# Modulation gates of a transformer block: from a matmul broadcast to a DRAM write and broadcast reads

## The chip, the cores and the metric

The kernel runs on one core of one Trainium2 chip. A core has five engines that each work through their own instructions in order: TensorE (PE: matmuls, and PEld, its weight loads), VectorE (DVE), ScalarE (ACT), GpSimd (POOL) and SyncE (SP, which here only issues transfers). The metric is the device time of one execution in microseconds (us).

## The reference

Input x is (4, 1024, 256) in float32, with a conditioning vector `mod` (4, 256) and a context of 77 tokens per batch. Two layers follow each other. The first is a block modulated by nine vectors per batch:

```python
m = silu(mod) @ w_ada + b_ada
sh_msa, sc_msa, g_msa, sh_mca, sc_mca, g_mca, sh_mlp, sc_mlp, g_mlp = [m[:, i*C:(i+1)*C][:, None, :] for i in range(9)]
x = x + g_msa * _self_attn(_ln(x) * (1 + sc_msa) + sh_msa, ...)         # windows of 128, 16 heads of 16
x = x + g_mca * _topk_cross_attn(_ln(x) * (1 + sc_mca) + sh_mca, ...)   # the 16 largest of 77 scores
x = x + g_mlp * _swiglu(_ln(x) * (1 + sc_mlp) + sh_mlp, ...)            # hidden width 1024
```

The second layer is another cross attention behind a layer norm with scale and bias from the same vector; it has no gate. The three gates g_msa, g_mca and g_mlp (each 256 numbers per batch) are what this change is about: each ends a branch with `h @ W + b`, so the kernel multiplies W's columns and b by the gate once per batch, and the branch then needs no product of its own.

## The kernel before

**Tiling.** The 4 batches are cut into 4 units of 256 rows (two row tiles of 128). Each of the 16 units passes five stages: self attention, selection (the 16 largest scores), cross attention, mlp, last attention. Units overlap: while one unit's selection keeps VectorE busy, another's mlp keeps PE busy.

**Order.** The program is written as a list of operations (`Plan.op`: engine, modelled cost, the closure that issues the instructions, buffers read and written, priority). `Plan.place` puts them one by one on the engines in modelled time, by priorities from hand-tuned tables, and gives every operation its buffers out of rings; `Plan.issue` then calls the closures in this order. So each engine's order is fixed when the program is built, and every engine runs its queue in that order; semaphores make an instruction wait for those on other engines whose results it reads or whose buffers it overwrites. The order depends on the modelled costs and the engine named in `op`, not on what a closure really issues.

**Start.** Before the first unit can run, the nine modulation vectors are made: `mod_group` (L690) makes shifts and scales as columns in the tile `mod` (added at L718), and `mod_gate` (L721) makes the three gates as rows: a matmul (L727) and VectorE's addition of the bias (L730) leave them in `gates`, a tile of 4 partitions (one for each batch) with 3 x 256 numbers. `context_columns` (copies by ScalarE at L755) and `context_kv` prepare keys and values of the context.

**The gates' way to 128 partitions.** `gated(b, pr)` (L1292) is called once for each batch b, and for each of three pairs of weights and bias: `w_so`, `w_co` (128 x 512 numbers each) and `w_m2` (128 x 2048). It

- loads the weights and the bias row, the latter broadcast to 128 partitions, by SP (L592);
- on PE, multiplies a broadcast column of the identity by `gates` (L1303), which writes row b of the gate to all 128 partitions of a PSUM bank (`mm`, a ring of two that nearly all matmul results go through; the profile shows two records for each of these matmuls, a pair);
- on ScalarE, copies the bank to the tile `gate` (L1306), a ring of two;
- on POOL, multiplies the bias row by it (L1308) and then the weights (L1310), in place.

That makes 12 matmuls, 12 copies and 24 multiplications in the whole kernel. The times at which the 12 matmuls start in the profiled execution (us): 34.45, 37.28, 38.95 and 42.1 (batch 0, and the first of batch 1), 89.9, 103.7, 117.5, 271.3, 336.1, 507.3, 527.8, 563.4.

**Other lines that the prediction speaks of.** In `normed` (layer norm): POOL's L907 and L909 (variance plus epsilon, power of -0.5: `rs`), VectorE's L912 (normalized rows), PE's transposes L919. In `self_attention`: the value projection L1075, scores and their shifts L1098 and L1104. In `shifts`: POOL's L961 (the first of four small operations on the negated row maxima `nm`, which VectorE's L996 makes), PE's transposes L970. In `norm` (softmax denominators): ScalarE's L1008, POOL's L1011 and L1023. L1049 (`add_row`) adds a gated bias row to x on POOL. L1162 is VectorE's sum in the selection stage.

Of the kernel before, what the change touches and what calls it, by code (L numbers as in the profile page):

```python
# [9 lines left out]
F32 = mybir.dt.float32  # L10
BF16 = mybir.dt.bfloat16
AF = mybir.ActivationFunctionType
ALU = mybir.AluOpType
# [3 lines left out]
P = 128  # L17
# [371 lines left out]
def tile_block(ctx: ExitStack, tc: tile.TileContext, a: dict, out: bass.AP):  # L389
    nc = tc.nc  # L390

    x_d, cond_d, ctx_d = a["x"], a["cond_1024"], a["ctx_1024"]
    B, L, C = x_d.shape
# [16 lines left out]
    def ctile(shape, name, dt=F32):  # L410
        return const.tile(shape, dt, tag=name, name=name)
# [7 lines left out]
    ident = ctile([P, P], "ident")  # L419
# [37 lines left out]
    pl = Plan()  # L457


    def f_pe(cols, n):  # L460
        return n * (cols * 0.00175 + 0.0095) + 0.1

    def f_act(n):
        return 0.21 + 0.00081 * n

    def f_dve(n):
        return 0.155 + 0.00104 * n

    def f_pool(n):
        return 0.13 + 0.00222 * n  # L470
# [7 lines left out]
    T_GATE = ("D", "D", 0.22, 0.05, 0.37, 0.216)  # L478
# [11 lines left out]
    def fixed(name, shape, dt=F32):  # L490
        return pl.fixed(ctile(shape, name, dt), name)
# [8 lines left out]
    n_mod = 26  # L500
    mod = fixed("mod", [P, n_mod, B])
    gates = fixed("gates", [B, 3, C])
    k_ctx = [fixed(f"k_{i}", [P, KC, B, 2, LC]) for i in range(2)]
    v_ctx = [fixed(f"v_{i}", [LC, B, H // 2, VP]) for i in range(2)]
    for v, fill in zip(v_ctx, (0.0, 1.0)):
# [7 lines left out]
    start, total = {}, 0  # L513
# [52 lines left out]
    bg_ada = at.buf("bg_ada", [B, 3, C])  # L566
# [22 lines left out]
    def load(buf, src, kb, prio, key=None, eng="SP", view=None):  # L589
        def fn():  # L590
            dst = buf() if view is None else view(buf())
            (nc.sync if eng == "SP" else nc.scalar).dma_start(dst, src)  # L592
        pl.op(eng, f_dma(kb) if eng == "SP" else 0.3, fn, w=[buf if key is None else (buf, key)],
              prio=prio, lag=2.0)
# [21 lines left out]
    for g, names in enumerate(groups):  # L616
        for name, hi in names:
            n, r = hi // P, n_rows[g]
# [11 lines left out]
    def chunk(name, lo, n, prio):  # L630
        c = pl.buf("chunk", f"{name}{lo}")
        load(c, a[name].rearrange("(kc p) n -> p kc n", p=P)[:, :, lo : lo + n], n, prio,
             view=lambda t: t[:, :, :n])
        early.append((chunk_lo, chunk_hi, c))
        return c
# [85 lines left out]
    def mod_gate(i, prio, dma_prio):  # L721
        c = chunk("L0_xcond_w_ada", (3 * i + 2) * C, C, dma_prio)
        pp = pl.buf("mm", f"modg{i}")

        def fn():
            for kc in range(KC):
                nc.tensor.matmul(pp()[:B, :C], sc_t()[:, kc, :B], c()[:, kc, :C],  # L727
                                 start=(kc == 0), stop=(kc == KC - 1))
        pl.op("PE", f_pe(C, 2), fn, w=[pp], r=[sc_t, c], prio=prio)
        pl.op("DVE", f_dve(256), lambda: nc.vector.tensor_tensor(  # L730
            gates()[:, i, :], pp()[:B, :C], bg_ada()[:, i, :], ALU.add), w=[(gates, i)], r=[pp, (bg_ada, i)], prio=prio)

    def filled(v):

# [55 lines left out]
    for i, key in enumerate("kqv"):  # L790
        weight(w_qkv, "L0_xcond_w_qkv", -84 + i, (1, 0, 2)[i] * C, C, key)
    mod_gate(0, -30, -79)
    mod_group("L0_xcond_w_ada", 3 * C, 6, False, -3, -70)
    load(cx, ctx_d.rearrange("b k c -> k b c"), 308, -69)
    weight(w_kv[0], "L0_xcond_w_kv", -68)
    weight(w_q0, "L0_xcond_w_q", -67)
    mod_gate(1, -2, -59)
    mod_group("L0_xcond_w_ada", 6 * C, 12, False, -1, -50)
    mod_gate(2, -1, -49)
    mod_group("L1_xcond_Wss_q", 0, 18, True, -1, -48)  # L800
    mod_group("L1_xcond_Wss_kv", 0, 22, True, -1, -47)
# [9 lines left out]
    for b in range(B):  # L811
        pl.op("DVE", 0.42, lambda b=b: nc.vector.bn_stats(st_c()[:LC, b, :], cx()[:, b, :]),
              w=[(st_c, b)], r=[cx], prio=-1)
    for b in range(B):
        pl.op("DVE", 0.16, lambda b=b: nc.vector.bn_aggr(mv_c()[:LC, b, :], st_c()[:LC, b, :]),
              w=[(mv_c, b)], r=[(st_c, b)], prio=-1)
# [475 lines left out]
    def gated(b, pr):  # L1292

        gw = {}
        for i, (key, name, kc) in enumerate(
            (("so", "L0_xcond_w_so", KC), ("co", "L0_xcond_w_co", KC), ("m2", "L0_xcond_w_m2", NF))
        ):
            first = None if b else DMA_FIRST[i]
            w, row = pl.buf("w_" + key, f"w_{key}{b}"), pl.buf("row", f"b_{key}{b}")
            gate, pg = pl.buf("gate", f"gate{b}{i}"), pl.buf("mm", f"pg{b}{i}")  # L1300
            load(w, a[name].rearrange("(kc p) n -> p kc n", p=P), 128 * kc, first or pr)
            load(row, a[f"L0_xcond_b_{key}"].partition_broadcast(P), 128, first or pr)
            pl.op("PE:gate", T_GATE, lambda i=i, pg=pg: nc.tensor.matmul(  # L1303
                pg()[:, :C], ident[:B, b : b + 1].to_broadcast([B, P]), gates()[:, i, :], start=True, stop=True),
                w=[pg], r=[(gates, i)], prio=pr, take=[gate])
            pl.op("ACT:gate", f_act(256), lambda gate=gate, pg=pg: nc.scalar.copy(gate(), pg()[:, :C]),  # L1306
                  w=[gate], r=[pg], prio=pr)
            pl.op("POOL:gate", f_pool(256), lambda row=row, gate=gate: nc.gpsimd.tensor_tensor(  # L1308
                row(), row(), gate(), ALU.mult), w=[row], r=[row, gate], prio=pr)
            pl.op("POOL:gate", f_pool(256 * kc), lambda w=w, gate=gate, kc=kc: nc.gpsimd.tensor_tensor(  # L1310
                w(), w(), gate().unsqueeze(1).to_broadcast([P, kc, C]), ALU.mult),
                w=[w], r=[w, gate], prio=pr)
            gw["b_" + key], gw["w_" + key] = row, w
        return gw

    stages = (self_attention, selection, cross_attention, mlp, last_attention)
    for b in range(B):
        pl.at = None
        gw = gated(b, b * NU - 0.5)
        for part in range(NU):  # L1320
            u = Unit()
            u.b, u.part, u.name = b, part, f"_{b}{part}"
            u.prio = float(b * NU + part)
            pl.at = None
            u.x = pl.buf("x", "x" + u.name)
            move_x(u, x_d, False)
            for k, stage in enumerate(stages):
                pl.at = (b * NU + part, k)
                u.prio = ORDER[b * NU + part][k]
                stage(u, gw)  # L1330
# [45 lines left out]
```

## Time and profile before

| | us |
|---|---|
| median of 3 runs (lowest, highest) | 1042.11 (1041.72, 1042.24) |
| the profiled execution's own time | 1041.43 |
| its span, from the first to the last instruction | 1039.4 |
| POOL's 12 multiplications L1308, each | 0.72 |
| POOL's 12 multiplications L1310: w_so and w_co, w_m2 | 1.26 to 1.27, 4.51 to 4.54 |
| the mean granted clock of PE over the span | 0.993 |

The page of the profile gives, in this order: each engine's busy time with its share of the span and the number of instructions; the span in 40 equal slices (26 us each here), one digit for each, in tenths; the transfers; the chain of work that ended last; and the costliest groups of instructions, with the idle time of the engine in front of them and what ended it. In a list of single instructions (the timeline) a line holds start, duration, engine, source line, operation, output<-inputs and shapes; a bracket at its end gives the engine's idle time in front of it and what released it. SPq is an issue in SP's queue. In the chain of waits a line holds start, duration, engine, tile and source line.

The only transfers of this kernel are issued by SP and, for a few small rows at the very start, by ScalarE; POOL issues none.

### The profile page before, as it was taken

How to read it: one execution, taken by the hardware profiler on the slowest of the kernel's cores; microseconds unless marked ns; L12 is line 12 of the kernel's file. 1: busy time of each engine (PE TensorE's matmuls, PEld its weight loads, DVE VectorE, ACT ScalarE, POOL GpSimd, SP SyncE). 2: the span in 40 equal slices, each digit the busy share in tenths (PEclk: the TensorE clock that was granted, in tenths of full speed). 3: DMA queues.
4: the chain of work that ended last, by engine and by line, in shares of the span. 5: the costliest groups of instructions: out<-in, count | busy, mean ns of one | idle time of the engine just before them, and what ended most of it. 6: DMA issues, size and time to landing. Idle time of an engine off the chain costs nothing.

```text
span 1039.4 us, 27476 instructions
## 1 busy us (share of the span) xinstructions
PE 1012.0 (97%) x10363; PEld 770.5 (74%) x10363; DVE 757.3 (73%) x4000; ACT 723.5 (70%) x1270; POOL 542.1 (52%) x751
## 2 busy tenths in 40 slices
PE   7899999999999999999999999999999999999997
PEld 5667777777777778777877777778767787778775
DVE  5177999979899999947833446599999977724232
ACT  3358786687687794758468667877688765764665
POOL 3384445466353573557635647546335464753653
PEclk9799999999999999999999999999999999999999
DMA  7710000001000000100000200000000001000000
GB/s 255 242 50 7 3 2 1 3 3 36 3 22 27 7 3 5 38 16 22 21 1 2 82 22 21 2 2 2 2 2 22 2 2 42 12 1 12 2 21 21
DMA packets 23623, 27.01 MB, mean 26 GB/s; under 512 B 1609, under 2 KB 20675, under 8 KB 23491
## 3 DMA queue, kind: packets, MB, share of 16 engines
q1 hardware_dynamic: 23455, 25.26, 7.7%
q8 instruction: 81, 1.33, 0.5%
q14 instruction: 52, 0.42, 0.1%
q10 hardware_dynamic: 35, 0.01, 0.0%
HBM read 21.07 MB, written 4.19 MB: 24 GB/s over the span
## 4 chain that ended last, share of the span: by engine, by line
PE 48%; DVE 13%; ACT 6%; POOL 2%; issue 1%; POOLq 0%; ACTq 0%; DVEq 0%
PE mm L1247 13%; PE mm L1275 8%; PE mm L938 5%; PE mm L1035 5%; PE s L1196 4%; PE o L1212 3%; PE s L985 3%; DVE share L1153 2%; DVE r L1147 2%; DVE nm L996 2%; PE s L1186 1%; DVE share L1145 1%; DVE share L1151 1%; PE mm L919 1%; ACT prob L1108 1%
## 5 line engine op out<-in xcount | busy, mean ns | idle before, releaser
L1247 PE MATMUL mm<-share,w_m 128*128 128x256 f32 x640 | 150.3, 386 | 0.4 <-ACT share L926 0.2
L1205 ACT ACTIVATE prob<-s 77x2048 f32<-77x2048 f32 x64 | 120.0, 1875 | 43.7 <-PE s L1201 43.4
L996 DVE TENSOR_REDUCE nm<-s 128x16 f32<-128x2048 f32 (+1 forms) x64 | 119.0, 1859 | 38.0 <-PE s L985 17.2
L1247 PEld LDWEIGHTS mm<-share,w_m 128*128 128x128 f32 x640 | 117.7, 190 | 26.0 <-issue 4.7
L1147 DVE MATCH_REPLACE8 r<-share 128x77 f32<-128x77 f32 x512 | 109.9, 222 | 0.0
L1145 DVE MAX8 share<-share 128x8 f32<-128x77 f32 x512 | 94.4, 225 | 21.0 <-ACT share L1138 21.0
L1153 DVE MATCH_REPLACE8 share<-share,r 128x77 f32<-128x77 f32 x512 | 109.6, 221 | 0.0
L1011 POOL TENSOR_TENSOR share<-share 128x256 f32<-128x256 f32 x64 | 47.1, 736 | 96.4 <-ACT share L1008 95.1
L1151 DVE MAX8 share<-r 128x8 f32<-128x77 f32 x512 | 93.9, 224 | 0.0
L1247 PE MATMUL mm<-slab,w_m 128*128 128x256 f32 x384 | 92.9, 388 | 0.7 <-ACT slab L926 0.5
L1023 POOL TENSOR_TENSOR slab<-slab,share 128x256 f32<-128x256 f32 x96 | 69.4, 730 | 28.4 <-ACT share L1018 19.2
L1261 POOL TENSOR_SCALAR slab<-slab 128x512 f32<-128x512 f32 x43 | 64.4, 1498 | 36.8 <-ACT slab L1259 33.0
L1247 PEld LDWEIGHTS mm<-slab,w_m 128*128 128x128 f32 x384 | 69.9, 190 | 15.6 <-issue 3.1
L1275 PE MATMUL mm<-share,slab 128*128 128x256 f32 x344 | 80.9, 381 | 0.0
L1008 ACT ACTIVATE share<-o,mask 128x256 f32<-128x256 f32 x128 | 66.6, 575 | 12.2 <-PE o L1212 9.6
L1108 ACT ACTIVATE prob<-s 128x2048 f32<-128x2048 f32 x32 | 60.5, 1889 | 17.9 <-PE s L1104 17.5
L1044 DVE TENSOR_TENSOR slab<-slab,mm 128x512 f32<-128x512 f32 x52 | 35.4, 680 | 50.9 <-PE mm L1035 25.7
L1275 PEld LDWEIGHTS mm<-share,slab 128*128 128x128 f32 x344 | 64.7, 190 | 10.0 <-issue 0.9
L1253 ACT ACTIVATE slab<-mm,cols 128x256 f32<-128x256 f32 x90 | 43.0, 480 | 41.0 <-PE mm L1247 40.5
L1212 PE MATMUL o<-prob,v 77*32 77x256 f32 x1024 | 67.9, 385 | 0.8 <-ACT share L1018 0.5
L1049 POOL TENSOR_TENSOR slab<-slab,row 128x512 f32<-128x512 f32 x39 | 49.9, 1278 | 28.5 <-DVE slab L912 15.4
L907 POOL TENSOR_SCALAR rs<-mv 128x2 f32<-128x2 f32 x64 | 14.2, 222 | 81.7 <-DVE mv L905 78.8
(183 smaller groups left out, 2427.0 us busy)
## 6 DMA issues: line engine op xcount, KB each, us to landing
share<-in_L_xcond_w_m_dram SPq DMA_DIRECT2D x4, 1024.0 KB
slab<-in_x_dram SPq DMA_DIRECT2D x9, 256.0 KB, 2.9
out_dram<-slab SPq DMA_DIRECT2D x9, 256.0 KB, 2.7
w_m<-in_L_xcond_w_m_dram SPq DMA_DIRECT2D x4, 512.0 KB, 6.8
share<-in_L_xcond_w_ada_dram SPq DMA_DIRECT2D x3, 512.0 KB, 3.8
w_so<-in_L_xcond_w_so_dram SPq DMA_DIRECT2D x4, 256.0 KB
w_co<-in_L_xcond_w_co_dram SPq DMA_DIRECT2D x4, 256.0 KB, 4.0
w_qkv<-in_L_xcond_w_qkv_dram SPq DMA_DIRECT2D x3, 256.0 KB
```

What stands on the lines that cost most here:

```text
L996: pl.op("DVE:max", f_dve(n), lambda: nc.vector.tensor_reduce(nm()[:, t], s4(), AX.X, ALU.max, negate=True), w=[(nm, t)], r=[s], prio=u.prio)
L1008: pl.op("ACT:nln", 0.5, lambda e=e, own=own, other=other: nc.scalar.activation(nz()[:, e, :], o()[:, ts(e, UT)], AF.Ln, bias=own, scale=ot ...
L1023: nc.gpsimd.tensor_tensor(dst, dst, shaped(nz()[:, k, :], dst), op)
L1108: pl.op("ACT:exp", f_act(2048), lambda s=s, prob=prob: nc.scalar.activation(prob(), s(), AF.Exp), w=[prob], r=[s], prio=pr)
L1145: nc.vector.max(top()[:, h + i, 0:8], sc()[:, h + i])
L1147: nc.vector.match_replace(r1()[:, i], top()[:, h + i, 0:8], sc()[:, h + i], NEG)
L1151: nc.vector.max(top()[:, h + i, 8:16], r1()[:, i])
L1153: nc.vector.match_replace(sc()[:, h + i], top()[:, h + i, 8:16], r1()[:, i], NEG)
L1205: pl.op("ACT:exp", f_act(2048), lambda s=s, prob=prob: nc.scalar.activation(prob()[:LC], s()[:LC], AF.Exp), w=[prob], r=[s], prio=pr)
L1212: nc.tensor.matmul(o()[r, :UT] if drops is not None else o()[r, ts(e, UT)], columns(v_z()[:, b], 8 * c + 2 * j + e), prob()[:LC, j, ts(e, ...
L1247: nc.tensor.matmul(pp()[:, ts(half, UT)], w_m1()[:, kc, m : m + P], ht()[:, kc, :], start=(kc == 0), stop=(kc == KC - 1))
L1275: nc.tensor.matmul(pp()[:, ts(t, C)], gts[f // 2]()[:, f % 2, ts(t, P)], w_m2()[:, f, :], start=(f == 0), stop=(f == NF - 1))
```

## The change

The PE closure in `gated` no longer issues a matmul, and ScalarE's copies are gone. In their place, each gate is written to outer memory as soon as VectorE has made it, and is read back from there to all 128 partitions straight into the tile `gate`; POOL issues both the writes and the reads.

```diff
@@ -500,6 +500,9 @@
     gates = fixed("gates", [B, 3, C])
+
+    dram = ctx.enter_context(tc.tile_pool(name="dram", bufs=1, space=bass.MemoryType.DRAM))
+    gates_d = [dram.tile([B, C], F32, tag=f"gates_d{i}", name=f"gates_d{i}") for i in range(3)]
@@ -727,8 +730,11 @@
-        pl.op("DVE", f_dve(256), lambda: nc.vector.tensor_tensor(
-            gates()[:, i, :], pp()[:B, :C], bg_ada()[:, i, :], ALU.add), w=[(gates, i)], r=[pp, (bg_ada, i)], prio=prio)
+
+        def add():
+            nc.vector.tensor_tensor(gates()[:, i, :], pp()[:B, :C], bg_ada()[:, i, :], ALU.add)
+            nc.gpsimd.dma_start(gates_d[i], gates()[:, i, :])
+        pl.op("DVE", f_dve(256), add, w=[(gates, i)], r=[pp, (bg_ada, i)], prio=prio)
@@ -1300,11 +1306,11 @@
-            pl.op("PE:gate", T_GATE, lambda i=i, pg=pg: nc.tensor.matmul(
-                pg()[:, :C], ident[:B, b : b + 1].to_broadcast([B, P]), gates()[:, i, :], start=True, stop=True),
+
+            pl.op("PE:gate", T_GATE, lambda i=i, gate=gate: nc.gpsimd.dma_start(
+                gate(), gates_d[i][b, :].partition_broadcast(P)),
                 w=[pg], r=[(gates, i)], prio=pr, take=[gate])
-            pl.op("ACT:gate", f_act(256), lambda gate=gate, pg=pg: nc.scalar.copy(gate(), pg()[:, :C]),
-                  w=[gate], r=[pg], prio=pr)
+            pl.op("ACT:gate", f_act(256), lambda: None, w=[gate], r=[pg], prio=pr)
```

Engines, costs, priorities and buffers named in `op` stay as they were, so the planned order is the same. In the instruction streams, PE loses 12 matmuls and ScalarE 12 copies; VectorE's and SP's stay as they are; POOL gains 15 issues of transfers, 3 writes (4 x 256 numbers) and 12 reads (256 numbers to 128 partitions). The reads stand in POOL's stream where the planner had put the matmuls in its modelled time. For batch 0 this gives: write 0, long before the rest; then writes 1 and 2; the read of gate 0, its row and w_so; the reads of gates 1 and 2; their row and w_co; an addition of a row to x (L1049); the first read of batch 1; w_m2 and its row. Of the later reads, most stand one to five instructions in front of the multiplication that uses them. Lines behind the change have numbers that are 3 higher (from L503 on) and 6 higher (from L736 on).

## The prediction

> **What bounds the kernel now.** I read the page first, then the chain of waits by window, then the timeline around each of the twelve places that the diff touches.
>
> ```profile
> PE 1012.0 (97%) x10363; PEld 770.5 (74%) x10363; DVE 757.3 (73%) x4000; ACT 723.5 (70%) x1270; POOL 542.1 (52%) x751
> ...
> PE   7899999999999999999999999999999999999997
> PEclk9799999999999999999999999999999999999999
> DMA  7710000001000000100000200000000001000000
> ```
>
> PE is busy nearly everywhere; POOL, which takes on the new work, half the time. But a busy PE need not set the end: for that I look at the chain. It can be followed back to about 300 us only, so only for the four gate matmul pairs after that (336, 507, 528 and 563 us) does it say which of them count. Two windows of the chain, start, us, what:
>
> ```profile
> 336.34 0.32 DVE zz L1162
> 336.66 2.20 DVE nm L996
> ```
>
> ```profile
> 527.88 0.62 PE mm L1303 x2
> 528.50 0.59 PE mm L919 x4
> ```
>
> At 336 us the chain is in VectorE's selection work, though L1303 runs on PE at 336.08; at 507 us too; at 563 us it is in ScalarE. Only the pair at 527.88 is a link. Before 300 us VectorE is busy 93.4 of 96 us (104 to 200) and 86.8 of 100 us (200 to 300), and the pairs at 89.9, 103.7 and 271.3 us are followed by a matmul that waits for ScalarE or VectorE in any case (0.33, 0.58 and 0.26 us). I count nothing there.
>
> The start is another matter. The windows table (us; PE, PEld, DVE, ACT, POOL busy; granted clock; DMA share; GB/s):
>
> ```profile
> 35.10:38.50 3.40, 2.50 (x11) 1.62 (x11) 0.00 (x0) 2.93 (x9) 1.94 (x2) 0.50 0.96 336
> 41.95:45.36 3.41, 3.41 (x15) 2.40 (x9) 0.00 (x0) 2.14 (x2) 3.23 (x2) 0.50 1.02 348
> 45.36:48.77 3.41, 3.41 (x36) 2.54 (x39) 1.27 (x3) 0.00 (x0) 2.17 (x2) 0.50 0.80 243
> 48.77:52.20 3.43, 3.43 (x63) 2.46 (x52) 1.03 (x6) 2.98 (x4) 0.11 (x1) 1.00 0.73 178
> ```
>
> From 35.1 to 48.77 us PE runs at half clock, without gaps from 38.9 on, VectorE waits for it (12.7 us for the matmul of L1075), and the transfers are saturated. Here PE sets the pace, and POOL and the transfers get new work in the same microseconds.
>
> **Removed: 12 matmul pairs (L1303) and 12 copies (L1306).** At full clock a pair is 0.6 us (0.62 on the chain), at half clock 0.9: L1104 ends at 42.31 and L1075 starts at 43.20; the pair at 38.95 stretches the 32 matmuls of L1098 to 2.92 us, where the next 32 take 2.04. The pairs at 34.45 and 37.28 lie in front of matmuls that wait for mod (L718) and for the bank that L755 empties until 38.45, so they are worth nothing. Start: 0.89 + 0.88 = **1.8 us** earlier at L1075. Chain at 528: **0.6 us**. The 12 copies (0.37 each) are off the chain in every window; what waits for them is POOL (22.4 us in six waits), which then waits for the transfer instead.
>
> **Added on POOL: 3 stores and 12 broadcast reads.** No instruction of before issues a transfer from POOL. Let c be POOL's time for one issue and l the time from its end until the data may be used. For c the nearest rows are SP's issue of a like row (0.34) and a POOL pass over 128x512 (1.27); I take 1.0, nearer to the POOL row, since POOL's cheapest pass over this very tile is 0.72. For l in quiet stretches there is a row: SP issues w_co at 331.22 for 0.37, POOL starts on it at 333.96, so l = 2.4. Under load, the bias rows land 4.6 us after issue (4.1 after its end), and one 9.3; those stand behind SP's own backlog, and the new queue has none, so I take 3.2, between 2.4 and 4.1.
>
> The transfer's cost is POOL's, since POOL runs in order: everything behind a multiplication that waits for its gate is late. Batch 0, POOL's new order: store 1, store 2, read 0, row, w_so, read 1, read 2, row, w_co, x + row (L1049), read of batch 1, w_m2, row. Store 0 goes out at 11.8 us, with POOL idle until 20.7: free. Store 2 can't start before VectorE's L730 ends (31.37). Issues on the path: store 2, read 0, read 1, read of batch 1 (4c; read 2 runs under the landing of read 1). Landings: read 0 and read 1 (2l). Work: 0.72 + 1.26 + 0.72 + 1.27 + 1.26 + 4.51 + 0.72 = 10.46. POOL is through at 31.37 + 10.46 + 4c + 2l = **41.8 + 4c + 2l** = 52.2 us. Before it was through at 47.5:
>
> ```profile
> 42.11 1.16 PE L1303 MATMUL mm<-gates,ident 4*128 4x256 f32 x2
> 43.20 3.78 PE L1075 MATMUL mm<-w_qkv,slab 128*128 128x256 f32 x8
> 46.80 0.72 POOL L1308 TENSOR_TENSOR row<-row,gate 128x256 f32<-128x256 f32 x1
> 52.09 0.73 POOL L1011 TENSOR_TENSOR share<-share 128x256 f32<-128x256 f32 x1 [4.56 <-ACT share L1008]
> 54.91 0.72 DVE L912 TENSOR_SCALAR slab<-slab,mv,rs 128x256 f32<-128x256 f32 x2
> ```
>
> The 4.56 us of idle time in front of L1011 are the cover. Behind it stand L1011, L907 and L909 (1.83 us with gaps), and VectorE's L912 at 54.91 needs them: POOL may be through at 53.1 without harm to the old times. With PE 1.8 us earlier, all of the start can move by min(1.8, 53.1 - 52.2) = **0.9 us**. So POOL eats half of what PE gives.
>
> Later the reads hit quiet transfers, and nine have different cover. POOL gaps take the issue, and with it most of the landing, at 101.5 (6.3 us), 268.4 (4.1) and 563.2 (2.4); at 521 us the 8.49 us wait for the copy covers all; at 506.8 the row is 1.8 us late but POOL idles 4.0 us at 513; the read at 91.7 has 3.0 us until its use, 0.4 short, and VectorE's selection goes on. Two have thin cover:
>
> ```profile
> 115.40 0.72 POOL L909 TENSOR_TENSOR rs<-rs,mhalf 128x2 f32<-128x2 f32 x1
> 118.71 0.73 POOL L1308 TENSOR_TENSOR row<-row,gate 128x256 f32<-128x256 f32 x1 [2.59 <-ACT gate L1306]
> 121.91 0.72 DVE L912 TENSOR_SCALAR share<-slab,mv,rs 128x256 f32<-128x256 f32 x2
> ```
>
> The row now starts at 116.12 + 1.0 + 2.4 = 119.5, 0.8 later; L909 behind it ended at 121.78, so L912 is 0.65 late. VectorE idles 13 us between 200 and 300, so I charge half: **0.3 us**.
>
> ```profile
> 331.22 0.37 SPq L592 DMA_DIRECT2D w_co<-in_L_xcond_w_co_dram  x1
> 333.96 1.27 POOL L1310 TENSOR_TENSOR w_co<-w_co,gate 128x512 f32<-128x512 f32 x1 [11.49 <-DMA w_co<-in_L_xcond_w_co_dram]
> 337.25 0.72 POOL L1308 TENSOR_TENSOR row<-row,gate 128x256 f32<-128x256 f32 x1 [2.02 <-ACT gate L1306]
> 338.93 0.21 POOL L961 CAST parts<-nm 128x32 bf16<-128x32 f32 x1 [0.96 <-DVE nm L996]
> ```
>
> Here it starts at 335.23 + 3.4 = 338.6, ends at 339.3, and L961, whose transposes (L970) are on the chain at 341.67, is **0.4 us** late.
>
> Sum: -0.9 - 0.6 + 0.3 + 0.4 = -0.8. The profiled execution took 1041.43 us (span 1039.4 and 2.0 around it), so 1040.6; it lies 0.7 below the median of 1042.11, by which the forecast is **1041.3 us**. One measurement of this kernel tells some 0.2%, 2.1 us, from no change.
>
> [...]
>
> **Rivals.**
> (B) The clock comes back one window earlier. The half clock lasts four steps of 3.41 us; without L1303 the step from 41.95 is nearly all dense L1075. For: PE loses its lightest matmuls there. Against: that step was already fully busy at 0.50. Worth 1.7 us, if POOL allows (c = 0.7, l = 2.6 puts it through at 49.8, 3.3 us ahead of 53.1): 1.8 + 0.6 + 0.9 of the 1.7 = 3.3, so 1038.8 us.
> (C) POOL overflows and the kernel is **slower**. Place: the two landings and four issues between 31.4 us and L1011. It decides from 4c + 2l = 11.3 on. For: the DMA share is 0.96 to 1.02 there. With c = 1.27, l = 4.1: through at 55.1, 2.0 us late, 0.5 + 0.7 at the two thin places, less 0.6: +2.6, 1044.7 us; each further us of l adds 2 (l = 6: 1048.5). Against: an own queue, without SP's backlog.
> [...]
>
> **Numbers.** Forecast (A) 0.38, its own range 1040.0 to 1043.0: 0.34 within 0.2%, 0.04 faster. B 0.18, faster. C 0.34: 0.31 slower, 0.03 within. D 0.10: 0.08 slower, 0.02 within. Together faster 0.22, within 0.39, slower 0.39. The bounds run from c = 0.34, l = 2.4 with B (-4.1: 1038.0) to c = 1.27, l = 8.9 (some +12.7: 1054.8); the range 1038.3 to 1047.5 leaves about 2 in 10 outside, mostly above.
>
> **What would show it.** POOL's issue rows give c, and the start of row after each gives l. L1075 should start at about 41.4, POOL's last row of batch 0 end near 52, L1011 stand right behind it without idle time. The clock's return at 45.4 instead of 48.8 is B. Late rows at 119.5 and 338.6 test the thin places. Wrong I am if L1011 comes after 53.1, if c exceeds 1.3, or if the early microseconds vanish in VectorE's queue before 300 us, which the chain does not cover.

## The result and the profile after

The changed kernel took **1047.82 us** (median of 4 runs, 1046.55 to 1049.0) against 1041.91 us before (4 runs beside it): 1.0056 times as long, 95% interval 1.0039 to 1.0074. In later runs (after, again, below) the ratio was 1.0079 (1.0066 to 1.0092). It is slower by some 6 to 8 us, and just above the predicted range, which ended at 1047.5. The profiled execution took 1049.0 us (span 1047.1).

Lines from the page after: busy times, the granted clock by slice, the new queue, and the reads (KB each, median us from issue to landing).

```profile
PE 1007.7 (96%) x10339; PEld 768.5 (73%) x10339; DVE 758.0 (72%) x4000; ACT 720.5 (69%) x1258; POOL 551.3 (53%) x766
...
PEclk9889999999999999999999999999999999999999
...
q0 software_dynamic: 672, 1.59, 0.6%
...
gate<-gates_d POOLq DMA_DIRECT2D x12, 128.0 KB, 3.4
```

PE has 4.3 us less work and POOL 9.2 us more, 15 issues of 0.52 to 0.76 us. The first slices of the clock row are the news: 979 before, 988 now. The wait view (POOL line waited for: total, times, longest) has

```profile
POOL row L1314 <- DMA gate<-gates_d: 24.0, 8, 5.6
```

Before, POOL waited 22.4 us in six waits for the copies. The total hardly moved; the place of the waits did. The timeline from 32 to 63 us (start, duration, instruction, idle time in front):

```profile
32.06 0.52 POOL L736 DMA_DIRECT2D gates_d<-gates  x1 [0.90 <-DVE gates L735]
32.57 0.59 POOL L1310 DMA_DIRECT2D gate<-gates_d  x1
38.70 0.72 POOL L1314 TENSOR_TENSOR row<-row,gate 128x256 f32<-128x256 f32 x1 [5.55 <-DMA gate<-gates_d]
...
40.60 1.14 POOL L1310 DMA_DIRECT2D gate<-gates_d  x2
47.33 0.73 POOL L1314 TENSOR_TENSOR row<-row,gate 128x256 f32<-128x256 f32 x1 [5.60 <-DMA gate<-gates_d]
...
55.53 0.72 POOL L1314 TENSOR_TENSOR row<-row,gate 128x256 f32<-128x256 f32 x1
56.22 0.71 POOL L1017 TENSOR_TENSOR share<-share 128x256 f32<-128x256 f32 x1
...
58.09 1.13 DVE L918 TENSOR_SCALAR slab<-slab,mv,rs 128x256 f32<-128x256 f32 x2 [5.41 <-POOL rs L915]
...
59.61 1.11 PE L925 MATMUL mm<-ident,slab 128*128 128x128 f32 x4 [5.72 <-DVE v L789]
62.22 3.13 PE L1081 MATMUL mm<-w_qkv,slab 128*128 128x256 f32 x8
```

Read it as a relay. Two landings of 5.5 us and more bring POOL's last row of batch 0 from 46.80 to 55.53. L1017, which had 4.56 us of idle time in front of it, has none and starts 4.1 us later than before (52.09). VectorE's L918 is 3.2 us late (54.91 before); in VectorE's queue it also holds up L789, which would empty a bank for PE. PE idles 5.72 us. And then L1081, which took 1.99 us before (as L1075), takes 3.13; L1041 starts at 69.19, 9.58 us behind the transposes L925. Before, the same way (L919 to L1035) took 7.75:

```profile
56.04 0.64 PE L919 MATMUL mm<-ident,slab 128*128 128x128 f32 x4
...
57.95 1.99 PE L1075 MATMUL mm<-w_qkv,slab 128*128 128x256 f32 x8
...
63.79 1.97 PE L1035 MATMUL mm<-w_so,slab 128*128 128x256 f32 x8 [0.39 <-POOL rs L907]
```

The windows table says why (busy us of PE, PEld, DVE, ACT, POOL; granted clock; DMA share; GB/s):

```profile
38.50:41.95 3.45, 1.83 (x30) 1.64 (x33) 0.00 (x0) 1.94 (x7) 3.03 (x4) 0.50 0.98 303
41.95:45.36 3.41, 3.41 (x36) 2.60 (x32) 0.00 (x0) 1.88 (x1) 0.00 (x0) 0.66 1.05 363
...
48.77:52.20 3.43, 3.43 (x43) 2.28 (x42) 1.69 (x7) 3.43 (x8) 3.41 (x4) 1.00 0.77 225
52.20:55.60 3.40, 1.69 (x8) 0.87 (x6) 0.42 (x1) 1.84 (x5) 3.40 (x2) 1.00 0.71 158
55.60:59.00 3.40, 0.00 (x0) 0.00 (x0) 0.91 (x2) 0.64 (x2) 2.97 (x5) 0.84 0.74 251
59.00:62.40 3.40, 2.79 (x9) 2.14 (x10) 2.29 (x10) 1.22 (x3) 3.10 (x3) 0.50 0.02 5
62.40:65.80 3.40, 3.40 (x12) 2.79 (x11) 1.30 (x5) 0.00 (x0) 3.13 (x6) 0.66 0.00 0
```

The clock does come back early, at 44.2 instead of 48.8 us: three steps of 3.41 us at half speed, not four. But after PE's idle time it is at half speed again for 6.8 us, two steps: PE pays twice for waiting.

VectorE runs the same instructions in both kernels, so the start of each can be compared one by one. The table gives how late one is against the profiled execution before, by its time there; every row is one profiled execution, and rows of kernels that begin alike differ by 1 to 2 us at 52 us (after and after, again: -2.3 and -4.2, with three and two steps of half clock at the start; last eight, which begins like the kernel before: +1.0).

| | 52 us | 75 us | 200 us | 310 us | 480 us | 600 us | end |
|---|---|---|---|---|---|---|---|
| after | -2.3 | +4.4 | +5.2 | +6.5 | +8.5 | +7.6 | +7.7 |
| after, again | -4.2 | +5.3 | +5.9 | +5.2 | +6.7 | +5.8 | +5.8 |
| gone | -3.4 | -3.4 | -3.5 | -3.5 | -3.1 | -3.9 | -3.9 |
| nobody waits | -3.8 | -3.8 | -3.9 | -4.7 | -4.0 | -4.5 | -4.5 |
| first four | -2.6 | +2.8 | +2.9 | +4.2 | +4.3 | +4.3 | +4.3 |
| last eight | +1.0 | +1.0 | +1.5 | +0.8 | +1.8 | +1.0 | +1.0 |
| three in a row | -3.8 | 0.0 | +0.5 | +1.8 | +2.7 | +2.2 | +2.1 |
| ahead | -2.2 | -0.9 | -1.0 | -1.0 | -0.4 | -1.0 | -1.0 |
| PE kept busy | -3.6 | +3.4 | +3.8 | +3.8 | +5.0 | +4.1 | +4.1 |
| ScalarE issues | +0.1 | +0.9 | +2.2 | +2.1 | +3.3 | +2.3 | +2.3 |
| direct | -0.3 | -0.6 | -0.7 | -1.4 | -1.0 | -1.5 | -1.4 |
| hybrid | -2.0 | -2.0 | -2.1 | -2.9 | -2.0 | -2.8 | -2.8 |

So at 52 us the changed kernel is ahead by 2.3 us, and by 75 us it is 4.4 behind. That is more than half of the loss, and the rest is in three places: 0.8 at 118 us, 1.4 near 295 us (a step of half clock, below) and 2.0 between 335 and 380 us, with 0.9 won back at 509 us.

### The profile page after: what moved, and what is told of

Its sections match the earlier page's. It is cut to its first block, busy times and chain, and to the rows that moved or that the text cites. A ratio compares the mean times of both kernels' runs of the same rounds, so it can differ in the third digit from the quotient of the medians.

```text
span 1047.1 us, 27433 instructions
## 1 busy us (share of the span) xinstructions
PE 1007.7 (96%) x10339; PEld 768.5 (73%) x10339; DVE 758.0 (72%) x4000; ACT 720.5 (69%) x1258; POOL 551.3 (53%) x766
## 4 chain that ended last, share of the span: by engine, by line
PE 44%; DVE 15%; ACT 5%; POOL 3%; issue 2%; DMA 1%; POOLq 0%; ACTq 0%; DVEq 0%
PE mm L1253 12%; PE mm L1281 7%; PE mm L944 5%; PE mm L1041 5%; PE s L1202 3%; PE s L991 3%; PE o L1218 3%; DVE r L1153 3%; DVE share L1159 3%; DVE share L1151 2%; DVE share L1157 2%; PE mm L925 1%; PE s L1192 1%; PE mm L1081 1%; DVE slab L918 1%
## 5 line engine op out<-in xcount | busy, mean ns | idle before, releaser
L1211 ACT ACTIVATE prob<-s 77x2048 f32<-77x2048 f32 x64 | 120.0, 1875 | 43.5 <-PE s L1207 43.2
L1017 POOL TENSOR_TENSOR share<-share 128x256 f32<-128x256 f32 x64 | 47.0, 735 | 91.1 <-ACT share L1014 86.7
```

The source lines that it names most:

```text
L1211: pl.op("ACT:exp", f_act(2048), lambda s=s, prob=prob: nc.scalar.activation(prob()[:LC], s()[:LC], AF.Exp), w=[prob], r=[s], prio=pr)
```

## The experiments

Theory: POOL waits for its own reads to land, one behind the other, while the transfers are saturated; the lateness goes on to VectorE and PE, and PE's idle time costs clock. Rivals: the removal itself (PE idles more and falls to half clock), the traffic and the issues, the eight later reads, the queue that issues. Ratios are to the kernel before on the same chip, with 95% intervals, from 5 to 12 runs. The experiments ran on three chips, on which the kernel before took 1041.84, 1041.83 and 1040.37 us; so kernels of different chips are compared by ratio.

**The removal alone** (before, with neither pairs nor copies nor transfers; the weights are multiplied by `one` in the same way):

```diff
-            pl.op("PE:gate", T_GATE, lambda i=i, pg=pg: nc.tensor.matmul(...
+            pl.op("PE:gate", T_GATE, lambda: None, ...
-                row(), row(), gate(), ALU.mult)
+                row(), row(), one, ALU.mult)
```

> The matmul pairs and the copies are gone and nothing stands in their place: POOL multiplies by a tile of ones instead of the gates, so the gates are left out of the result. Theory (the change loses because POOL waits for its own reads to land): what the removal alone is worth must be a gain, by the 2.3 us that PE is ahead at 50 us in the changed kernel and up to 0.6 us at 528 us: 1038.5 to 1040.0 us, PE's half clock from about 34 us for three windows. Rival (without the pairs PE idles more, falls to half clock at other times, and that is the loss): 1045 us or more, with a second stretch of half clock after 54 us though POOL is on time.

1037.73 us, ratio 0.9960 (0.9947 to 0.9974): a gain of 4.1 us, more than the theory gave. Its windows:

```profile
35.10:38.50 3.40, 0.75 (x8) 0.62 (x9) 0.24 (x2) 2.56 (x8) 0.00 (x0) 0.75 1.02 358
38.50:41.95 3.45, 3.40 (x52) 2.87 (x52) 0.00 (x0) 0.91 (x3) 0.00 (x0) 0.50 0.80 256
41.95:45.36 3.41, 3.41 (x42) 2.69 (x44) 0.42 (x1) 1.34 (x1) 2.72 (x1) 0.76 0.96 345
```

Half clock is down to 6.8 us (0.25 and 0.24 of a window at the sides stand for half of each, 1.7 us), two steps where there were four, and 3.4 us are won by 52 us. The rival is out: less work for PE at the start does not make it fall to half clock more.

**All transfers, nobody waits** (after, multiplying by ones; rows and weights; the gates stay in `bg_ada`'s tile, and the reads go to four tiles):

```diff
-                gate(), gates_d[i][b, :].partition_broadcast(P)),
+                gate_t[(3 * b + i) % 4], gates_d[i][b, :].partition_broadcast(P)),
-                row(), row(), gate(), ALU.mult)
+                row(), row(), one, ALU.mult)
```

> All 15 transfers of the change are issued by POOL at the same places and go to their tiles, but POOL multiplies by ones, so nobody waits for a read to land (the gates are left out of the result). Theory (the landing waits are the loss): 1039.5 to 1041.5 us, POOL's last row of batch 0 ends before 49 us, no second stretch of half clock. Rival (the traffic takes bandwidth from the loads while the transfers are saturated, or POOL's 15 issues are the cost): 1045 us or more, nearly the changed kernel's time.

1038.55 us, ratio 0.9965 (0.9952 to 0.9979), 1 us below the theory's range. Its POOL timeline:

```profile
32.46 0.59 POOL L1314 DMA_DIRECT2D gate<-gates_d  x1
33.06 0.74 POOL L1318 TENSOR_TENSOR row<-row,one 128x256 f32<-128x256 f32 x1
...
43.53 4.53 POOL L1320 TENSOR_TENSOR share<-share,one 128x2048 f32<-128x2048 f32 x1 [1.24 <-DMA share<-in_L_xcond_w_m_dram]
48.03 0.72 POOL L1318 TENSOR_TENSOR row<-row,one 128x256 f32<-128x256 f32 x1
```

The row starts right behind the issue, and POOL is through at 48.75 instead of 56.25. The same 15 issues and the same bytes cost under 1 us beside the removal alone, although POOL still waits 0.47 and 1.96 us for the stores of gates 1 and 2 to land before it can issue their reads. The waits for the reads, with what they set off, are the other 9 us. This settles the main question.

**Which reads** (a condition chooses the read or, behind `else`, matmul and copy; `>= 4` for the last eight):

```diff
+            if 3 * b + i < 4:
...
+            else:
...
```

> Only the first four gates (batch 0 and the first of batch 1, all needed before 62 us) are read back by POOL; the other eight go by matmul and copy as before. Theory (most of the loss is at the start): at 100 us it is 3.9 to 4.4 us behind the kernel before, and ends there: 1045.5 to 1046.5 us. Rival (the eight later reads, at places with thin cover, are most of the loss): below 1043.5 us.

1045.31 us, ratio 1.0034 (1.0021 to 1.0046). Nearly as expected; behind by 2.8 us at 75 us rather than 4, with one step of half clock after PE's idle time instead of two.

> The reverse: the first four gates go by matmul and copy as before, the other eight are read back by POOL. Theory: no loss before 100 us, +0.8 us at 120 us, +2.0 us between 330 and 380 us, -0.9 us between 500 and 520 us: 1043.5 to 1044.5 us. Rival (the later steps appear only because the start was late): within 0.7 us of the kernel before.

1042.08 us, ratio 0.9989 (0.9972 to 1.0006): a miss of the theory's number; the rival's is met. The losses at 118 (0.6) and between 335 and 380 us (1.1) do appear, but 0.8 before 310 and 0.9 at 509 us are won back: the eight later reads are worth nothing on balance. The rival's reason (they lose only behind a late start) is not right either, since two of the losses are there though this start is late by 1.0 us only.

**Keep PE busy while it waits** (after, ahead of the transposes L925 at 59.61 us):

```diff
+            if scale_at == 2 and u.name == "_01":
+                for _ in range(20):
+                    nc.tensor.matmul(banks_s[:, 0, :P], ident, ident, start=True, stop=True)
```

> The changed kernel, with 20 matmuls of the identity into a PSUM bank that is free, ahead of L925 at 59.61 us, so that PE has work while it waits for POOL's lateness to pass. Theory: the second stretch of half clock (57.9 to 64.7 us) does not come, and of its 6.8 us at half speed 1.1 to 2.4 us are saved: 2.0 to 3.3 us behind the kernel before at 70 us instead of 4.4, 1045.0 to 1046.5 us in all. Rival (the clock costs nothing since POOL and VectorE set the pace there): same as the changed kernel, 1047 to 1048.5 us.

1045.58 us, ratio 1.0033 (1.0019 to 1.0047), against 1047.82 and 1.0056 of the changed kernel; ten of the twelve runs are below the lowest of the changed kernel's nine. PE's timeline (two records for each matmul):

```profile
52.41 4.63 PE L925 MATMUL s<-ident 128*128 128x128 f32 x40
59.13 0.66 PE L928 MATMUL mm<-ident,slab 128*128 128x128 f32 x4 [2.10 <-DVE v L789]
...
61.15 3.20 PE L1084 MATMUL mm<-w_qkv,slab 128*128 128x256 f32 x8
```

Work that computes nothing makes the kernel some 2 us faster. The half clock is not gone (2.1 us of idle time are left), but it is one step instead of two. Only a part of the gain is seen at this place: PE takes 9.06 us from the transposes to L1044 (L1041 after the change) instead of 9.58. After's profiled execution also has the step near 295 us (1.4 us), which this one lacks.

Over the profiled executions, PE's idle time just in front of these transposes, the steps of half clock behind it, and PE's time from there to L1041 go together: 8.13 us, three steps, 10.05 us (after, again); 5.72, two, 9.58 (after); 5.40, 3.38 and 2.10, one each, 8.69, 9.04 and 9.06 (first four, three in a row, PE kept busy); 1.65 and 1.06, none, 7.60 (ahead, ScalarE issues).

**Another queue issues** (`nc.scalar.dma_start` for the 12 reads):

> The changed kernel with its 12 reads issued by ScalarE instead of POOL, at the same places of the planned order; the stores stay on POOL. Theory (it is the landing that POOL waits for, and it is as long from another queue while the transfers are saturated): 1046 us or more, and ScalarE, which now waits for the stores to land and for the tile to come free, is late too. Rival (POOL's queue is what makes the reads slow to land): landings under 4.2 us at the start, POOL through before 53 us, 1043 us or less.

1044.45 us, ratio 1.0030 (1.0015 to 1.0046): neither number. The landing is no shorter. The read of gate 0 is issued at 34.81 (0.37 us; lines of ScalarE's queue and of POOL):

```profile
34.81 0.37 ACTq L1310 DMA_DIRECT2D gate<-gates_d  x1
...
42.05 0.72 POOL L1314 TENSOR_TENSOR row<-row,gate 128x256 f32<-128x256 f32 x1 [9.85 <-DMA gate<-gates_d]
45.70 0.72 POOL L1314 TENSOR_TENSOR row<-row,gate 128x256 f32<-128x256 f32 x1 [1.71 <-DMA gate<-gates_d]
```

That is 6.9 us from the issue's end. POOL is through 2.2 us sooner than after the change, since gate 1's read no longer stands behind POOL's work on gate 0: it goes out at 36.56, and though it lands 8.8 us after the end of its issue (45.70 less 36.92), most of that lies beside the landing of gate 0. So here the overlap of the landings gained time, and the other queue did not shorten them.

**Overlap the landings** (after, with five gate tiles; then also without batch 1's second and third read in the start):

```diff
+            def reads(b=b):
+                for k in range(3):
+                    nc.gpsimd.dma_start(gate_t[(3 * b + k) % 5], gates_d[k][b, :].partition_broadcast(P))
+            pl.op("PE:gate", T_GATE, reads if i == 0 else lambda: None, ...
```

> As the changed kernel, with five gate tiles (the gates stay in the tile that held their biases, which frees the room), and all three reads of a batch are issued in a row where its first one stood, so that the landings run side by side and the later reads are issued well ahead. Theory (POOL's landing waits, one behind the other, are the loss): POOL waits for the stores of gates 1 and 2 to land (about 37.8 us), gate 1 lands near 42.5, POOL is through with batch 0 near 53 us instead of 56.2: 0 to +1 us against the kernel before at 100 us, nothing lost at 118 and 337 us, 1040.0 to 1042.5 us in all. Rival (more reads at once in the saturated stretch only make each land later): 1045 us or more.

1041.63 us, ratio 0.9998 (0.9984 to 1.0012): as the theory gave, and POOL is through at 52.4. But 0.6 us at 118 and 0.9 between 335 and 380 us are still lost, where the theory gave nothing.

> As the kernel with three reads in a row, but of batch 1 only the first read is issued at the start; the other reads of a batch, and the first of the next one, go out together where the second stood. Theory: two issues and 256 KB fewer before w_m2's multiplication, POOL through near 51.5 us: 1 to 2 us ahead of three reads in a row, 1038.5 to 1041.0 us. Rival: as before, 1045 us or more.

1040.15 us, ratio 0.9977 (0.9963 to 0.9992): faster than both kernels. Its POOL timeline:

```profile
37.60 0.54 POOL L1316 DMA_DIRECT2D gate<-gates_d  x1 [1.49 <-DMA gates_d<-share]
...
43.34 0.73 POOL L1320 TENSOR_TENSOR row<-row,gate 128x256 f32<-128x256 f32 x1 [3.22 <-DMA gate<-gates_d]
...
51.54 0.73 POOL L1320 TENSOR_TENSOR row<-row,gate 128x256 f32<-128x256 f32 x1
```

POOL now waits for the stores of gates 1 and 2 to land before it can issue their reads, and is through at 52.3: two landings in a row are left, the store's and the read's.

**Without the second landing.** Straight from the tile to all partitions, in `mod_gate`; or, in the second kernel, gates 1 and 2 by matmul and copy as before:

```diff
+            nc.gpsimd.dma_start(gate_t[i], bg_ada()[0:1, i, :].unsqueeze(1).to_broadcast([1, P, C]))
```

> As the kernel with reads ahead, but batch 0's three gates are broadcast straight from the tile in which VectorE makes them, by a transfer from one partition to all 128, issued right behind VectorE's addition; outer memory serves batches 1 to 3 only. Theory (two landings one behind the other, store and then read, still hold POOL until 52 us in the kernel with reads ahead): gates 1 and 2 land by 38 us, POOL is through near 49 us, 1038.0 to 1039.5 us, close to the kernel in which nobody waits (1038.55). Rival (128 reads of one partition land much later than reads of outer memory): gate 1 lands after 44 us, 1041 us or more.

1039.17 us, ratio 0.9996 (0.9983 to 1.0009), not told from the kernel before, which ran at 1040.37 on this chip. Gate 1 is there at 38.27, as the theory gave; gate 2 landed only at 43.2, 11.5 us after its issue began. w_m2's load lands later still, 2.7 us later than in the run where nobody waits (its multiplication starts at 46.19, not 43.53), and POOL is through at 51.4. Whether 128 reads of one partition delay the loads was not tried, but the traces point that way: from 32 to 40 us the DMA engines are as busy in both runs (shares of 1.00 to 1.05), and move 219 and 251 GB/s here against 344 and 332 where nobody waits (mean of 32 to 36 and of 36 to 40 us).

> As the kernel with reads ahead, but gates 1 and 2 of batch 0 come by matmul and copy as before the change; the other ten are read back. Theory: POOL waits for one landing only and is through near 49 us, while PE does two pairs at half clock again (0.9 us each, and up to one window of half clock more): 1039.5 to 1041.0 us. Rival (PE's pairs at the start are what costs, whatever POOL does): 1041.8 us, the kernel before, or more.

1038.01 us, ratio 0.9982 (0.9974 to 0.9991): faster than the theory's range, and the lowest median of a kernel that computes the whole. By its ratio it is not told from reads ahead (0.9977, on another chip). POOL:

```profile
39.66 0.72 POOL L1324 TENSOR_TENSOR row<-row,gate 128x256 f32<-128x256 f32 x1 [6.87 <-DMA gate<-gates_d]
40.35 1.25 POOL L1326 TENSOR_TENSOR w_so<-w_so,gate 128x512 f32<-128x512 f32 x1
41.57 0.72 POOL L1324 TENSOR_TENSOR row<-row,gate 128x256 f32<-128x256 f32 x1
...
49.82 0.73 POOL L1324 TENSOR_TENSOR row<-row,gate 128x256 f32<-128x256 f32 x1
```

One wait for a landing, no wait for gate 1, through at 50.5. Two of PE's pairs are back and cost little: its half clock lasts three steps.

> The changed kernel itself, beside the others on one chip. Both theories: 1046.5 to 1049 us; it gives the interval against which the next ones are read, and shows how much of it is runs with more stretches of half clock (a lower mean granted clock).

1048.43 us (5 runs, 1046.71 to 1050.07), as expected.

## Why the prediction was wrong

- **The step that failed** is the value of l: "the new queue has none, so I take 3.2, between 2.4 and 4.1". The rows behind the reads started 5.5 and 6.1 us after the end of their issues (38.70 less 33.16; 47.33 less 41.20). That is 5.3 us more than two landings of 3.2. The nearest row was the bias rows' 4.1 us under the same load, and I argued it down by a property of the queue that no row showed. ScalarE's queue, another one without SP's backlog, took 6.9 and 8.8.
- **Rival C named what happened**, place and point: it decides from 4c + 2l = 11.3 on. With c = 0.57, the mean of the four issues, and the two landings it is 2.3 + 11.6 = 13.9, and 41.8 + 13.9 = 55.7; POOL was through at 56.25. The rest is about the 0.7 us by which store 2 began late (32.06, not 31.37). c was mis-sized the other way (1.0 for 0.57), worth 1.7 us.
- **C's price was too low.** POOL through at 56.25 is 3.2 us late; with 1.2 at the thin places and 0.6 back that is 3.8 us, and the profiled execution ended 7.7 late. Missing are 1.2 us at the start (VectorE's L918 is 3.2 us late, and at 75 us it is 4.4), 1.4 us at the step of half clock near 295 us, and 1.6 us at the thin places (0.8 and 2.0 for 1.2); 0.9 came back instead of 0.6. No term of the forecast or of C had half clock behind a wait of PE: the wait was taken at its length. It was followed by two steps, and PE took 9.58 us for the work of 7.75. I had the four steps in front of me and used them only for a gain (B).
- **The gain was too low as well.** 1.8 us by the pairs' own time is right: in the removal alone L1075 (there L1077) starts at 41.30 instead of 43.20. (After the change it starts at 42.86, since ScalarE's copy that PE waits for in front of it came later.) But the removal alone gives 3.4 by 52 us, because two steps of half clock go. Rival B's early return of the clock is real in the runs without these pairs, with one step less (after, first four, ahead) or two, and POOL did not let it through.
- **0.6 us at 528 us**: not there. The removal alone has a step of 0.96 us at 509 us and none at 528. It comes from VectorE's pair L912, before and (as L914) in the removal alone:

```profile
508.90 1.69 DVE L912 TENSOR_SCALAR share<-slab,mv,rs 128x256 f32<-128x256 f32 x2
```

```profile
505.85 0.73 DVE L914 TENSOR_SCALAR share<-slab,mv,rs 128x256 f32<-128x256 f32 x2
```

Before, POOL's L1310 runs from 509.06 to 510.43, in the middle of the pair, whose second instruction takes 1.36 us from 509.22; without the copy it starts earlier (there L1309, 504.37 to 505.64), ahead of the pair, which takes 0.73 us for 1.69. In the whole trace before, 74 of the 128 instructions of L912 have no tensor instruction of POOL beside them, and each took 0.40 to 0.42 us; of the 54 with one beside them, eight took 1.20 to 1.37. That a link on the chain is worth its length failed here: what stood behind it took its place. In the removal alone the chain there runs over 1.88 us of ScalarE (L1207, at 523.14).
- **Thin places.** At 118 us the row came 3.6 us after the read's issue began (120.47 to 124.08), 3.4 forecast, and all of the delay counted: 0.8, not half of 0.65. At 337 us the read is on the chain, as forecast:

```profile
342.80 3.47 DMA gate<-gates_d
...
346.35 0.72 POOL row L1314
```

It cost 1.0 us at that place instead of 0.4, and 1.0 more came in the same stretch, 0.4 of which the removal alone has too. The last eight reads together came out at zero.
- **Issues that stretch beside a busy VectorE** (D, 0.10) are shown by no run: the 12 reads' issues took 0.54 to 0.66 us each, with VectorE busy for 92.65 of the 96 us from 104 to 200 and for 97.31 of the 100 us from 300 to 400. Nor is VectorE behind the long landings at the start: it is not busy at all from 38.5 to 45.4 us, while gate 1's read is on its way.

What stays open: the step of half clock near 290 to 297 us, in after, first four and three in a row. PE waits twice for ScalarE there, 1.03 and 0.48 us in after and 1.03 and 0.49 before, where no step follows. In after both waits lie in the 3.41 us ahead of it (290.0 to 293.4 us, PE busy for 1.90 of them); before, PE was busy for 1.99 us in the 3.41 us that hold most of them (284.3 to 287.7, in steps counted on from the clock's return at 48.76). What decides between the two is not known.

## What to carry to other kernels

The broadcast through outer memory took 4.3 us of work off PE here and put 24.0 us of waiting for landings on POOL, which uses the result. In POOL's queue two landings stood one behind the other (through with batch 0 at 56.25); with the three reads issued ahead of the first use it was through at 52.4. Price a landing by the slowest row under the same load, not by the quiet one: from the issue's end, gates 0 and 1 of batch 0 took 5.5 and 6.1 us here while the transfers were saturated (6.9 and 8.8 when ScalarE issued them), and after's eight reads from 95 us on 2.6 to 2.9. And price an idle PE by the clock it loses afterwards: 5.7 us of waiting were followed by two steps of half speed, which cost PE 1.8 us, and the kernel with empty work in the gap was some 2 us faster.

## What the runs showed of the hardware

- Half clock came in steps of 3.41 us. By the clock records it lasted 13.65 us before (from 35.11 us) and 10.24, 6.83 and 3.41 us after (from 33.99, 57.89 and 293.41): four, three, two and one times 3.41; after's stretches of full clock between them, 13.65 and 228.69 us, are 4 and 67 times 3.41. The removal alone had two steps at the start. The single runs of the kernel before (1039.3 to 1047.2 us over three chips) follow their mean granted clock: 1039.3 to 1041.4 us at 0.994 and 0.995, 1041.0 to 1042.4 at 0.993, 1044.5 to 1046.3 at 0.990, some 0.9 us for each 0.001. One step lowers the mean over 1039 us by 0.0016 (half of 3.41), so by an estimate from these numbers much of this kernel's scatter goes with how many steps a run gets.
- An issue of a 128 KB read took POOL 0.54 to 0.66 us and ScalarE 0.33 to 0.37; under load its landing was no faster from ScalarE (6.9 and 8.8 us from the issue's end, 5.5 and 6.1 from POOL).
- Under load batch 0's reads both started and moved late. By the packets in after's trace, the reads of gates 1 and 2 began 2.9 us after the end of the first one's issue, and both together moved for 3.1 us; the reads from 95 us on began after 0.7 to 1.0 us and moved for 1.3 to 1.6.
- After the change POOL's stores of 4 KB landed 5.2 to 5.8 us after their issue began, batch 0's reads of 128 KB 6.1 to 6.7.
